# The order of a state-space mixer's block: weighted values and the next x's transposes behind the gate, the store behind the convolution

## The chip, the cores and the metric

The kernel runs on one core of a Trainium2 chip. The metric is the device time of one execution in microseconds, taken as the median of several runs. Five engines work side by side: TensorE (PE in the profile, with its weight loads as PEld), VectorE (DVE), ScalarE (ACT), GpSimd (POOL) and SyncE (SP). Each engine takes its instructions in the order in which they stand in its queue, and waits on semaphores for what other engines and DMA transfers produce. In this kernel SyncE issues nearly all transfers, and ScalarE's queue issues one kind, the store of a block's result.

## The reference

The network is one layer of four parts: causal attention with 32 heads and an adapter, a gated linear layer ("ffn"), a state-space mixer, and the ffn again, each behind a layer norm and added to x. The input is (4, 256, 512) in float32. The change lies in the mixer, which is cut here to what matters:

```python
proj = input_states @ in_proj_w.T             # gate 8192, x 8192, B 1024, C 1024, dt 128
xBC = silu(causal_conv4(xBC) + conv_b)        # four taps per channel
dt = softplus(dt + dt_bias); cum = cumsum(dt * A)
# 128 heads of 64; B and C are shared by the 16 heads of a group (8 groups)
y = (C B^T, causal, times exp(cum_i - cum_j)) @ (dt * x) + D * x
g = y * silu(gate)
g = g * rsqrt(mean over the group's 1024 channels of g*g + eps) * norm_w
out = g @ out_w.T
```

## The kernel before

Channels are taken 128 at a time: a block is two heads, 64 blocks in all (`NB`), eight to each of eight groups (`GB`, `G`). In block i, g is its group and gi its place in the group. All 1024 tokens (four sequences of 256) lie along the free axis, so a block's arrays are 128x1024.

A large product is done as three products of split operands (`mm3`, lines 115 to 117: upper by upper, upper by lower, lower by upper). An upper part is a cast on ScalarE, a lower part a subtraction on VectorE; both are named "lowering" and "copy" below.

The function `block(i)` (line 1513) issues the work of one block. Nothing is planned by costs: the instructions stand on each engine in the order in which the code calls them. The steps, with the names of the profile:

- x projection: 24 matmuls into `pp`, in two halves of 12 (`projected("x", i)`).
- `decays(i - 1)`: on ScalarE the exponentials of the decays of the block before, in `em` (lines 1205 to 1213), after which the next rows of cumulated sums are fetched (`rows`, L1178).
- `turn(i - 1)`: eight transposes of the former block's x on TensorE into two PSUM banks (`trx`, L1225), multiplied by dt on VectorE into `xd` (L1228). It stands between the two halves of the x projection.
- `weigh(i - 1)`: VectorE multiplies `em` by the scores `gm` (L1218).
- `conv` and `taps`: ScalarE's first tap (L962), then three on VectorE (L972).
- `squared(i - 2)`: the square of an older result on ScalarE (L1274, L1276), added up on GpSimd (L1277).
- `outer`: 24 matmuls of the output product of the group before, for one tile of tokens (`pog`), in blocks that have one; VectorE adds the result to x (`scaled`, L1373).
- `side_by_side`: the SiLU of the convolution (L1144), which makes the block's x; it needs a table load on ScalarE first.
- `inner_products(i - 1)`: `product`, 32 pairs of small matmuls into `pyy` (L1244), and `finish`, which is `gated` on VectorE (L1256, L1259): the block's result `gb`.
- gate projection: 24 matmuls, then `gate(i)` on ScalarE (L1435).
- `differences(i)` on VectorE (L1193, L1194): the exponents for the next block's `decays`.

In blocks with an output product ahead of the gate, `inner_products(i - 1)` stands between that product and the gate projection; in others (group 0, the first block of group 1, and each second block, gi = 1) it stands behind the gate projection.

The result `gb` is stored in DRAM (`spilled(i - 2)`, L1265) by ScalarE's queue at the head of block i, and read back (`fetch_half`, `gr`, L1341, on SyncE's queue) once a group is whole. In the second block of a group the last block of the former group is stored; the read-back of its half waits for that store. In the same block that half is cast (`upper_half`, L1351), four blocks of output weights are copied (`upper_out`, L1298, from `wor`, L1291), and behind the block the sums of squares (`pqs`, L1314), the first output product and a small transpose (`trq`, L1326) follow on TensorE. In ScalarE's queue the cast and the copies stand ahead of the block's `side_by_side`:

```python
if g and gi >= 1:
    ss = {1: (1,), 2: (4, 5)}.get(gi, (2 * gi, 2 * gi + 1))
    lower.extend(upper_half(g - 1, s) for s in ss)
if g and gi == 1:
    lower.extend(upper_out((g - 1) * GB + k) for k in range(4, 8))
g_steps = projected("g", i)
xs2[i] = side_by_side(acc)
```

In the fourth and fifth blocks (gi = 3, 4) the B and C projections of the next group follow the gate (24 matmuls each); in the seventh (gi = 6) the next group's scores are made (`scores`, `pg`, L1162).

PSUM has eight banks: four for two `pp`, two for `pyy`, and two shared by `trx`, `pog`, `pg`, `pqs` and `trq` (tag "m"). There is one `xd`, so a block's xd can be written only when the former product has read it.

Of the kernel before, what the change touches and what calls it, by code (L numbers as in the profile page):

```python
# [79 lines left out]
def hybrid_kernel(  # L80
# [788 lines left out]
    def mixer(feed, ps, mnorm, later):  # L869
        with ExitStack() as es, ExitStack() as inner:  # L870
# [391 lines left out]
            def spilled(n, gb):  # L1262

                if n < NB - 1:
                    nc.scalar.dma_start(spill[(n // GB) % 2][n % GB], gb)  # L1265
                else:
                    last.append(gb)

            def squared(n, x2, gb):

                g = n // GB
                if g not in sqs:
                    sqs[g] = p2.tile([P, NT], F32, name="sq", tag="sq", bufs=1)
                    nc.scalar.activation(sqs[g], gb, AF.Square)  # L1274
                else:
                    nc.scalar.activation(x2, gb, AF.Square)  # L1276
                    (nc.gpsimd if n < NB - 2 else nc.vector).tensor_tensor(sqs[g], sqs[g], x2, ALU.add)  # L1277
# [130 lines left out]
            def fetch_half(q, s):  # L1408
                halves[q, s] = recall(q, s // 2, s % 2)
# [20 lines left out]
            xs2, gts, ems, xds, gbs = {}, {}, {}, {}, {}  # L1430
# [10 lines left out]
            def turn(i):  # L1441
                xds[i] = turned(i, xs2[i])
# [5 lines left out]
            def inner_products(i):  # L1448
                finish(i, product(xds.pop(i), ems.pop(i)))

            def finish(i, py):
                gbs[i] = gated(i, xs2[i], gts.pop(i), py)
# [60 lines left out]
            def block(i):  # L1513

                g, gi = divmod(i, GB)
                n = at["x", i]
                lower = []  # L1520

                def lowered():
                    for f in lower:
                        f()
                    lower.clear()

                out = (g - 1, gi - 1) if gi else (g - 2, TT - 1)
                if out[0] < 0:  # L1530
                    out = None
                first_out = gi == 1

                if i >= 2:
                    spilled(i - 2, gbs[i - 2])
                if g and gi == 1:
                    fetch_half(g - 1, 1)
                    fetch_half(g - 1, 2)
                if late_:
                    nc.vector.reciprocal(rgs[g - 1], rgs[g - 1])  # L1540
                    scaled(*late_.pop())
                if g and gi == 2:
                    upper_half(g - 1, 3)()
                x_steps = projected("x", i)
                next(x_steps)
                pp = next(x_steps)
                waiting = [k for k in "bc" if k + "pp" in group]

                def begun_next(k):
                    group[k] = conv(group[k + "pp"], (NB if k == "b" else NB + G) + g + 1, False)  # L1550

                def ended_next(k):
                    taps(group[k], group.pop(k + "pp"), (NB if k == "b" else NB + G) + g + 1)


                for k in waiting if g == 0 else ():
                    begun_next(k)
                    ended_next(k)


                between = out is None
                decays(i - 1, (0,) if between else (0, 1))
                for k in waiting if g else ():
                    begun_next(k)
                turn(i - 1)
                if between:
                    weighted(ems[i - 1][0], gms[(i - 1) // GB])
                else:
                    weigh(i - 1)
                for k in waiting if g else ():  # L1570
                    ended_next(k)
                next(x_steps)
                acc = conv(pp, i, True)
                if between:
                    decays(i - 1, (1,))
                    taps(acc, pp, i, which=(0, 1))
                    weighted(ems[i - 1][1], gms[(i - 1) // GB])
                    taps(acc, pp, i, which=(2,))
                else:
                    taps(acc, pp, i)  # L1580
                if i >= 2:
                    squared(i - 2, xs2.pop(i - 2), gbs.pop(i - 2))
                done = outer(*out) if out and not first_out else None
                lower.append(upper_piece(n + 2))
# [7 lines that stand above are left out]
                for k in waiting:  # L1592
                    silu(group[k])
                if done:
                    scaled(*done)
                lowered()

                both = i == NB - 1
                scoring = None

                def scored():
                    nonlocal scoring
                    if gi == 6 and g + 1 < G:
                        scoring = scores(group.pop("b"), group.pop("c"))
                        gms[g + 1] = next(scoring)
                        next(scoring)
                        next(scoring)

                next(g_steps)
                for _ in pending:  # L1610
                    for _ in pending.pop():
                        pass
                if done and not both:
                    inner_products(i - 1)
                    pp = next(g_steps)
                    scored()
                    next(g_steps)
                else:
                    pp = next(g_steps)
                    next(g_steps)  # L1620
                    scored()
                    if both:
                        return last_block(i, pp)
                    inner_products(i - 1)
                lower.append(upper_piece(n + 3))
                if g and gi == 0:
                    lower.append(upper_half(g - 1, 0))
                    lower.extend(upper_out((g - 1) * GB + k) for k in range(4))
                if g and gi == 1:
                    lower.append(upper_half(g - 1, 2))  # L1630
                ems[i] = [differences(h) for h in (2 * i, 2 * i + 1)]
                lowered()
                if scoring and g:
                    for _ in scoring:
                        pass
                elif scoring:
                    pending.append(scoring)
                if gi == 6:
                    for k in range(4):
                        fetch_out(g * GB + k)  # L1640
                if g == 0 and gi == 7:
                    fetch_half(0, 0)
                gate(i, pp)
                if g and first_out:
                    r = sums(g - 1)
                    late_.append(outer(*out))
                    rgs[g - 1] = root(sums_turned(r))
                if gi in NEXT and g + 1 < G:
                    group[NEXT[gi] + "pp"] = whole(projected(NEXT[gi], g + 1))
                    upper_piece(n + 4)()  # L1650
# [13 lines left out]
            def last_block(i, pp):  # L1664

                g = i // GB
                py = product(xds.pop(i - 1), ems.pop(i - 1))
                done = outer(G - 2, TT - 1)
                for k in range(3):
                    fetch_out(NB - 3 + k)  # L1670
                ems[i] = [differences(h) for h in (2 * i, 2 * i + 1)]
                made(0, 0)()
                gate(i, pp)
                decays(i, (0,))
                lower = [upper_out(g * GB + k) for k in range(4)]
                lower.append(made(1, 0))
                for f in lower[:2]:
                    f()
                scaled(*done)
                for f in lower[2:]:  # L1680
                    f()
                weighted(ems[i][0], gms[g])
                finish(i - 1, py)
                decays(i, (1,))
                made(2, 0)()
                turn(i)
                weighted(ems[i][1], gms[g])
                spilled(i - 1, gbs[i - 1])
# [6 lines left out]
            i = NB - 1  # L1695
# [208 lines left out]
```

## Time and profile before

| what | value |
|---|---|
| median of 3 runs | 1811.24 us (1810.67 to 1813.12) |
| profiled execution, its own time | 1812.82 us |
| its span, first to last instruction | 1811.0 us |
| mean granted TensorE clock | 0.994 |
| PE busy | 1754.1 us, 97% of the span |
| DVE busy | 1439.5 us, 79% |
| ACT busy | 1268.4 us, 70% |
| POOL busy | 250.9 us, 14% |
| moved by DMA | 169.51 MB, mean 94 GB/s |

The table comes from the page of the profile. Busy time of an engine is the time in which it has an instruction in hand; matmuls overlap, so 97% says that there is always one in flight. A timeline row gives the start, the duration, the engine, the source line, the operation, the tiles (out<-in), the shape, how many instructions are merged, and in brackets the idle time before it and what ended that. The letter q behind an engine's name marks its queue, which issues transfers.

### The profile page before, as it was taken

How to read it: one execution, taken by the hardware profiler on the slowest of the kernel's cores; microseconds unless marked ns; L12 is line 12 of the kernel's file. 1: busy time of each engine (PE TensorE's matmuls, PEld its weight loads, DVE VectorE, ACT ScalarE, POOL GpSimd, SP SyncE). 2: the span in 40 equal slices, each digit the busy share in tenths (PEclk: the TensorE clock that was granted, in tenths of full speed). 3: DMA queues.
4: the chain of work that ended last, by engine and by line, in shares of the span. 5: the costliest groups of instructions: out<-in, count | busy, mean ns of one | idle time of the engine just before them, and what ended most of it. 6: DMA issues, size and time to landing. Idle time of an engine off the chain costs nothing.

```text
span 1811.0 us, 32937 instructions
## 1 busy us (share of the span) xinstructions
PE 1754.1 (97%) x12734; PEld 1425.0 (79%) x12734; DVE 1439.5 (79%) x2547; ACT 1268.4 (70%) x2289; POOL 250.9 (14%) x253
## 2 busy tenths in 40 slices
PE   8999988899999999999999999999999999999998
PEld 6777767778877888888888888888888888888877
DVE  6676677888998788878878797878787878887777
ACT  6666675487888667766866686768667866777754
POOL 6332230110110011011101111110111001101100
PEclk9999999999999999999999999999999999999999
DMA  4000000113243334423432343335323433343231
GB/s 151 1 1 1 23 15 26 43 59 106 94 134 125 105 94 135 134 76 103 162 109 93 94 146 99 100 94 170 99 93 104 154 105 94 111 140 112 85 98 57
DMA packets 134381, 169.51 MB, mean 94 GB/s; under 512 B 12240, under 2 KB 77520, under 8 KB 134224
## 3 DMA queue, kind: packets, MB, share of 16 engines
q1 hardware_dynamic: 125152, 134.37, 24.3%
q10 hardware_dynamic: 9072, 33.03, 4.8%
q8 instruction: 100, 1.64, 0.4%
q14 instruction: 57, 0.47, 0.1%
HBM read 131.71 MB, written 35.65 MB: 92 GB/s over the span
## 4 chain that ended last, share of the span: by engine, by line
PE 79%; DVE 10%; ACT 7%; issue 2%; POOL 1%; DMA 1%; SPq 0%; ACTq 0%; DVEq 0%; POOLq 0%
PE pp L115 14%; PE pp L117 13%; PE pp L116 13%; PE pyy L1244 8%; PE pog L115 6%; PE pog L116 6%; PE pog L117 6%; PE trx L1225 3%; PE ptr L521 1%; ACT e L505 1%; DVE acc L972 1%; PE pq L115 1%; PE pg L1162 1%; PE pq L116 1%; DVE eT L522 1%
## 5 line engine op out<-in xcount | busy, mean ns | idle before, releaser
L115 PE MATMUL pp<-mx,w 128*128 128x512 f32 x1144 | 459.3, 401 | 0.0
L117 PE MATMUL pp<-mx,w 128*128 128x512 f32 x1144 | 446.7, 391 | 0.0
L116 PE MATMUL pp<-mx,w 128*128 128x512 f32 x1144 | 446.1, 390 | 0.0
L1277 POOL TENSOR_TENSOR sq<-sq,x 128x1024 f32<-128x1024 f32 x54 | 132.1, 2446 | 1177.8 <-ACT x L1276 1177.8
L117 PEld LDWEIGHTS pp<-mx,w 128*128 128x128 f32 x1144 | 214.8, 188 | 46.2
L115 PEld LDWEIGHTS pp<-mx,w 128*128 128x128 f32 x1144 | 214.8, 188 | 44.6
L972 DVE SCALAR_TENSOR_TENSOR acc<-pp,cw_s,acc 128x1012 f32<-128x1012 f32 (+2 forms) x192 | 244.6, 1274 | 4.3
L116 PEld LDWEIGHTS pp<-mx,w 128*128 128x128 f32 x1144 | 215.2, 188 | 40.4
L1218 DVE TENSOR_TENSOR em<-em,gm 128x1280 f32<-128x1280 f32 x128 | 189.5, 1489 | 72.1 <-ACT em L1213 72.1
L115 PE MATMUL pog<-wo,gh 128*128 128x512 f32 x512 | 200.7, 392 | 1.9 <-DVE x L1373 1.9
L117 PE MATMUL pog<-wo,gh 128*128 128x512 f32 x512 | 199.7, 390 | 0.9 <-DVE gh L1356 0.9
L116 PE MATMUL pog<-wo,gh 128*128 128x512 f32 x512 | 199.4, 389 | 0.0
L1228 DVE TENSOR_TENSOR xd<-trx,dt_t 128x512 f32<-128x512 f32 x128 | 82.4, 686 | 141.4 <-PE trx L1225 141.4
L1144 ACT ACT_TABLE_LOAD x63 | 80.8, 1283 | 138.8 <-DVE acc L972 138.7
L1435 ACT ACTIVATE gt<-pp 128x1024 f32<-128x1024 f32 x64 | 65.6, 1025 | 145.2 <-PE pp L117 145.2
L1244 PEld LDWEIGHTS pyy<-em,xd 64*64 64x64 f32 x4096 | 130.2, 133 | 44.2 <-issue 17.3
L1205 ACT ACTIVATE em<-r,end_t 128x128 f32<-128x128 f32 x512 | 163.0, 389 | 0.8
L1244 PE MATMUL pyy<-em,xd 64*64 64x256 f32 (+3 forms) x4096 | 157.8, 300 | 3.1 <-DVE em L1218 2.9
L115 PEld LDWEIGHTS pog<-wo,gh 128*128 128x128 f32 x512 | 96.1, 188 | 24.7 <-issue 2.7
L117 PEld LDWEIGHTS pog<-wo,gh 128*128 128x128 f32 x512 | 96.1, 188 | 22.2 <-DVE gh L1356 2.1
L116 PEld LDWEIGHTS pog<-wo,gh 128*128 128x128 f32 x512 | 96.1, 188 | 19.4
L505 ACT ACTIVATE e<-e,nmx 128x256 f32<-128x256 f32 (+1 forms) x256 | 96.6, 450 | 19.9 <-DVE nmx L496 19.3
(323 smaller groups left out, 3131.8 us busy)
## 6 DMA issues: line engine op xcount, KB each, us to landing
wr<-in_win_dram SPq DMA_DIRECT2D x144, 256.0 KB, 2.8
r<-cumd SPq DMA_DIRECT2D x256, 128.0 KB, 2.9
spill<-gb ACTq DMA_DIRECT2D x63, 512.0 KB, 2.8
gr<-spill SPq DMA_DIRECT2D x120, 256.0 KB, 3.5
wor<-in_wout_dram SPq DMA_DIRECT2D x64, 256.0 KB, 4.5
out_dram<-x SPq DMA_DIRECT2D x7, 256.0 KB, 2.6
x<-in_x_dram SPq DMA_DIRECT2D x1, 1536.0 KB, 8.8
gr<-spill SPq DMA_DIRECT2D x8, 192.0 KB, 2.5
```

The costliest lines, as they stand in the source:

```text
L115: nc.tensor.matmul(o, lh, rh, start=(first and k == 0), stop=False)
L116: nc.tensor.matmul(o, lh, rl, start=False, stop=False)
L117: nc.tensor.matmul(o, ll, rh, start=False, stop=(last and k == n - 1))
L505: nc.scalar.activation(es_[c][:, 2 * j + pr, :], es_[c][:, 2 * j + pr, :], AF.Exp, scale=-1.0, bias=nm[:, j : j + 1],)
L972: nc.vector.scalar_tensor_tensor(av[:, :, d:], pv[:, :, : L - d], cw_s[:, ch, tap : tap + 1], av[:, :, d:], ALU.mult, ALU.add,)
L1144: nc.scalar.activation(pair(x2).rearrange("p k u i -> p u k i"), acc.rearrange("p (u k i) -> p u k i", u=2, i=Q), AF.Silu,)
L1205: nc.scalar.activation(piece(e, j, c, 2 - c, 2), rv[:, j, 2:, :], AF.Exp, bias=end_t[:, 2 * j + c, h : h + 1],)
L1218: nc.vector.tensor_tensor(e, e, gm, ALU.mult)
L1228: nc.vector.tensor_tensor(xd[:, hs, :].rearrange("p c (h d) -> p c h d", h=2), tr.rearrange("p c (h d) -> p c h d", h=2), dt_t[:, hs, 2 * ...
L1244: nc.tensor.matmul(py[d, u, j * L + c * Q : (j + 1) * L].rearrange("p (k i) -> p k i", i=Q), xd[us, 4 * j + c, d], piece(es2[hh], j, c)[us ...
L1277: (nc.gpsimd if n < NB - 2 else nc.vector).tensor_tensor(sqs[g], sqs[g], x2, ALU.add)
L1435: nc.scalar.activation(gts[i], pp, AF.Silu)
```

## The change

Three things change in `block`. First, `turn` is called for the block's own x at the end of the block, directly behind `product(i - 1)`, rather than for the former block's x between the halves of the x projection. Second, `product(i - 1)` stands behind the whole gate projection in every block, and `finish` behind `turn`; on VectorE the order at the end of a block is now `differences`, the xd products, the gating. Third, the store of block i - 2, and in each second block the two read-backs behind it, are called behind the taps; on ScalarE's queue the store then stands directly behind the convolution, ahead of the square.

```diff
-                if i >= 2:
-                    spilled(i - 2, gbs[i - 2])
-                if g and gi == 1:
-                    fetch_half(g - 1, 1)
-                    fetch_half(g - 1, 2)
                 if late_:
...
-                turn(i - 1)
+                if i == 2:
+                    turn(i - 1)
                 if between:
...
                     taps(acc, pp, i)
                 if i >= 2:
+                    spilled(i - 2, gbs[i - 2])
+                    if g and gi == 1:
+                        fetch_half(g - 1, 1)
+                        fetch_half(g - 1, 2)
                     squared(i - 2, xs2.pop(i - 2), gbs.pop(i - 2))
...
-                if done and not both:
-                    inner_products(i - 1)
-                    pp = next(g_steps)
-                    scored()
-                    next(g_steps)
-                else:
-                    pp = next(g_steps)
-                    next(g_steps)
-                    scored()
-                    if both:
-                        return last_block(i, pp)
-                    inner_products(i - 1)
+                pp = next(g_steps)
+                next(g_steps)
+                scored()
+                if both:
+                    return last_block(i, pp)
+                py = product(xds.pop(i - 1), ems.pop(i - 1))
...
                 ems[i] = [differences(h) for h in (2 * i, 2 * i + 1)]
+                turn(i)
+                finish(i - 1, py)
                 lowered()
```

## The prediction

> **What bounds the kernel now.** I read the page first, then the timeline of TensorE in a plain block of the mixer, then ScalarE, SyncE and TensorE in the block where a group's sums fall due.
>
> ```profile
> PE 1754.1 (97%) x12734; PEld 1425.0 (79%) x12734; DVE 1439.5 (79%) x2547; ACT 1268.4 (70%) x2289; POOL 250.9 (14%) x253
> PE 79%; DVE 10%; ACT 7%; issue 2%; POOL 1%; DMA 1%; SPq 0%; ACTq 0%; DVEq 0%; POOLq 0%
> ```
>
> TensorE (PE) is busy for 97% of the span and carries 79% of the chain that ended last. There is little idle time to win back: the question is whether the new order opens holes in it.
>
> ```profile
> 910.76 0.39 PE L117 MATMUL pog<-wo,gh 128*128 128x512 f32 x1
> 911.08 2.41 PE L1244 MATMUL pyy<-em,xd 64*64 64x256 f32 x64
> 913.42 0.50 PE L115 MATMUL pp<-mx,w 128*128 128x512 f32 x1
> 913.75 0.39 PE L116 MATMUL pp<-mx,w 128*128 128x512 f32 x1
> ...
> 921.49 0.40 PE L117 MATMUL pp<-mx,w 128*128 128x512 f32 x1
> 921.72 1.04 PE L1225 MATMUL trx<-con,x 128*128 128x128 f32 x8
> 922.51 0.48 PE L115 MATMUL pp<-mx,w 128*128 128x512 f32 x1
> 922.83 0.40 PE L116 MATMUL pp<-mx,w 128*128 128x512 f32 x1
> ```
>
> Large matmuls start every 0.227 us without a break. The weighted values (L1244) and the transposes (L1225) are two inserts between them.
>
> The third reading is the second block of group 3 (i=25). Its x projection starts at 878.48 on TensorE. Call that s.
>
> ```profile
> 878.74 0.33 ACTq L1265 DMA_DIRECT2D spill<-gb  x1
> 886.36 1.19 ACT L962 ACTIVATE acc<-pp,cb_s,cw_s 128x1024 f32<-128x1024 f32 x1
> 889.29 0.62 ACT L1351 CAST gh<-gr 128x512 fp32r<-128x512 f32 x1 [0.28 <-DMA gr<-spill]
> 889.82 2.56 ACT L1298 ACTIVATE wo<-wor,nw_s 128x512 fp32r<-128x512 f32 x4
> 892.39 1.28 ACT L1144 ACT_TABLE_LOAD   x1
> 893.68 1.06 ACT L1144 ACTIVATE x<-acc 128x1024 f32<-128x1024 f32 x1
> ```
>
> ```profile
> 879.59 2.31 SPq L1291 DMA_DIRECT2D wor<-in_wout_dram  x4
> 882.73 0.93 SPq L1341 DMA_DIRECT2D gr<-spill  x2
> ```
>
> ```profile
> 890.35 2.41 PE L1244 MATMUL pyy<-em,xd 64*64 64x256 f32 x64
> 892.69 0.64 PE L1314 MATMUL pqs<-sq,ones 128*32 128x256 f32 x8
> 898.98 0.47 PE L115 MATMUL pp<-mx,w 128*128 128x512 f32 x1
> ```
>
> The last block of the former group is stored (spill), read back (gr), and cast (L1351); only behind that cast and four copies of output weights does ScalarE compute the SiLU that makes x, ending at 894.74, s+16.26. The read-back ended ScalarE's wait already: it has no slack here. TensorE has, because it transposes this x only in the next block, at 901.82.
>
> **The change, part by part.**
>
> *The two inserts made neighbours.* Now: pog to pyy 0.32, pyy to pp 2.34, first pp 0.33; pp to trx 0.23, trx to pp 0.79, first pp 0.32: 4.33 over six steps. Together: 0.32 + 2.34 + 0.79 + 0.32 = 3.77 over four, and two ordinary steps of 0.227: 4.22. That is 0.106 us saved in each of the 47 blocks that have an output product ahead of the gate: -5.0. No row shows pyy directly before trx; the bounds are 0 and that saving. [...]
>
> *Waits that vanish.* The view of L1225's waits has "DVE x L1373: 4.3, 4": transposes that found no free PSUM bank behind the late output product. They now run before that product: -4.3 (0 to -4.3).
>
> *Plain blocks (those 47).* x(i) is now transposed at the end of block i, after 72 large matmuls (16.34) and pyy (0.09 + 2.34): s+18.8, where s is always the block's first x matmul. Before, SiLU ended at s+15.9 (914.83 against 898.98). It comes earlier now: the gate no longer waits for pyy, so it starts some 3 us before s, and gate, table load and exponentials (0.93, 1.29, 5.33) end by s+4.5. What moves on VectorE: the two xd products (done at s+1.55) and the gating (2.6) stand ahead of one lowering (0.6), weighing (2.8) and taps (3.75, begun at 908.50): taps end at s+11.3, and SiLU, 1.29 and 1.06 later, at s+13.7. No wait, with 5 us of cover; without the cover each 1 us would cost 47.
>
> *Second blocks (gi=1), groups 2 to 7: the cost.* There is no output product ahead of the gate, so TensorE wants x after 48 matmuls (10.90), 0.09 and 2.34: s+13.33. SiLU is nowhere near. The store now stands behind the convolution on ScalarE's queue. x's last matmul is readable 0.42 after its issue, as the gate shows (918.77 to 919.19): 23 x 0.227 + 0.42 = s+5.64; the store follows by 0.06: s+5.70. Store to read-back issue takes 878.74 to 882.73 = 3.99: s+9.69. Behind the read-back on SyncE's queue stand later weight loads, which have time. Read-back to cast took 6.56 here; the page's median for gr is 3.5. The four loads of 256 KB that stood ahead of it still do, so I take 5.3: s+15.0. Cast to SiLU's end is 889.29 to 894.74 = 5.45: s+20.45. The transposes wait 7.1 (with 3.5 and 6.56: 5.3 and 8.4), and all behind them on TensorE: the sums, the output product, the next block. Then pqs (L1314) needs a PSUM bank that both transposes hold until xd is written; xd's first half starts 0.64 behind the transposes (921.72 to 922.36) and takes 0.64, against 0.79 of transposes: +0.6. Six blocks x 7.7 = +46.2 (35 to 54).
>
> [...]
>
> *Second block of group 1.* Block 8 has no output product, so ScalarE is behind when block 9 starts: SiLU's end s-1.0, two copies 1.0, four weight copies 2.56, gate 0.93, table load 1.29, exponentials 5.33: convolution at s+10.1. Then 0.06 + 3.99 + 5.3 + 5.45: s+24.9. The rest of the block (0.79, 0.6, 0.57 for pqs, 5.45, 0.3) ends at s+32.6; before it took 23.29 (527.83 to 551.12): +9.3 (5 to 12).
>
> *Group 0.* Blocks there have no output product (48 matmuls, 10.90, and 3.4 for the inserts), so x decides: x projection 5.64, convolution to SiLU's end 432.17 to 441.31 = 9.14, 0.1, transposes 0.79: 15.67 a block. Seven with two extra projections of 5.45 make 120.6 against 118.03 (421.83 to 539.86): +2.6 (-2 to +6).
>
> *Seventh blocks.* The second half of the scores needs the banks that the transposes hold: +0.6 in groups 1 to 6: +3.6 (0 to 5).
>
> *TensorE's clock.*
>
> ```profile
> 247.00:249.00 2.00, 0.04 (x1) 0.00 (x0) 0.00 (x0) 2.00 (x7) 0.00 (x0) 1.00 0.00 0
> 249.30:252.60 3.30, 3.30 (x18) 2.86 (x18) 2.47 (x7) 0.85 (x2) 0.00 (x0) 0.50 0.00 0
> ```
>
> These stretches (columns: PE busy first, granted clock third from the end) are of the attention: 2.19 us without a matmul, then the granted clock is 0.50, and back at 1.00 by 252.8. At half clock 3.4 us lose 1.7. Seven waits of 7 us or more ought to bring this: +11.9 (0, or 24 if the stretch is twice as long). [...]
>
> Sum: -5.0 - 4.3 + 46.2 + 9.3 + 2.6 + 3.6 + 11.9 = +64.3. The profiled execution took 1812.82 (span 1811.0, 1.8 around it), so 1877.1; it stood 1.58 over the median of 1811.24, so 1875.5 against the median. I say 1875.
>
> **The rivals.** *The store is not what ends last.* If the read-back lands early, VectorE still sets SiLU: from s, xd to 1.55, gating to 4.15, three lowerings (0.6, 0.6, 2.65) to 8.0, weighing to 10.8, taps to 14.5, table and SiLU to 16.9. The wait is 3.5, so six blocks at 4.1 and group 1 at 5 make 29.6; with -9.3, +2.6, +3.6 it is +26.5: 1838, or 1850 with the clock's 11.9. For it: by the page store and read-back land in 2.8 and 3.5 at the median. Against: the cast already waited for the read-back.
>
> *Faster.* TensorE wants x in a second block at s+13.33; if SiLU ends by then, nothing waits, and the saved seams and bank waits remain: -9.3, 1802. It decides at the cast: it must start by s+7.9, and the store leaves ScalarE at s+5.70 at the earliest. For it only the earlier gate; against it the 3.99 of the store alone.
>
> *x late in every block.* VectorE is 79% busy; if xd and the gating ahead of the weighing pushed taps out by over 5 us, every plain block would wait, at 1 us each 47 more: about 1922. Against: the steps that VectorE has in such a block add up to some 15.5 us of the 19.8 between its last output matmuls (910.76 to 930.55).
>
> **How the numbers follow.** Forecast 0.72, store not last 0.13, x late everywhere 0.07, faster 0.05, cancelling to nothing 0.03. With every term at its lower or upper bound at once the forecast would be 1840 or 1912; the range 1838 to 1900 takes in the first rival and most of the forecast's, and leaves out some 0.2. About 0.2% (3.6 us) is what this measurement can tell from no change: faster 0.05, same 0.03, slower 0.92.
>
> **What would show it.** Right: in the second block of each group TensorE's largest wait, by transposes (L1225) for x (ACT L1144), about 7 us; casts (L1351) waiting for gr; a granted clock below 1 there; plain blocks still without holes, some 0.1 us shorter. Wrong: transposes that start at s+13.4 in second blocks, or waits of them in plain blocks, or a second-block wait of 3.5 with no wait for gr.

## The result, and the profile after

The changed kernel takes 1870.65 us at the median (1865.88 to 1872.15), the kernel before 1811.47 in the same series (four runs, three of them those of the table above): a ratio of 1.0316 (95% interval 1.0301 to 1.033). The change costs 59 us; 64 were predicted. The profiled execution took 1869.54, with a span of 1867.8 and a mean granted clock of 0.981 (0.994 before).

The page first: the busy line and the chain of the changed kernel.

```profile
PE 1760.0 (94%) x12734; PEld 1431.6 (77%) x12734; DVE 1438.7 (77%) x2547; ACT 1273.3 (68%) x2289; POOL 265.7 (14%) x253
PE 71%; DVE 11%; ACT 10%; DMA 4%; issue 3%; POOL 1%; SPq 0%; ACTq 0%; DVEq 0%; POOLq 0%
```

TensorE has the same number of instructions and nearly the same busy time (1754.1 before), spread over a longer span. Of the chain it has lost 8 of 79 points, to ScalarE (7 to 10), DMA (1 to 4), VectorE and issue: TensorE now stands still while others finish. The view of waits of the changed kernel (total us, times, longest) says for what:

```profile
PE trx L1225 <- ACT x L1144: 50.2, 11, 9.0
ACT gh L1351 <- DMA gr<-spill: 43.0, 9, 5.8
```

Before, the view had no line like the first, and the second had 4.3 us. The block to read is again the second block of group 3; its x projection starts at s = 896.68. ScalarE, SyncE and TensorE in the timeline of the changed kernel:

```profile
902.46 1.21 ACT L962 ACTIVATE acc<-pp,cb_s,cw_s 128x1024 f32<-128x1024 f32 x1 [0.65 <-PE pp L117]
902.52 0.33 ACTq L1265 DMA_DIRECT2D spill<-gb  x1
...
910.56 0.62 ACT L1351 CAST gh<-gr 128x512 fp32r<-128x512 f32 x1 [5.43 <-DMA gr<-spill]
911.09 2.56 ACT L1298 ACTIVATE wo<-wor,nw_s 128x512 fp32r<-128x512 f32 x4
913.66 1.28 ACT L1144 ACT_TABLE_LOAD   x1
914.95 1.06 ACT L1144 ACTIVATE x<-acc 128x1024 f32<-128x1024 f32 x1
```

```profile
906.65 0.93 SPq L1341 DMA_DIRECT2D gr<-spill  x2
```

```profile
907.79 2.41 PE L1244 MATMUL pyy<-em,xd 64*64 64x256 f32 x64
916.06 1.97 PE L1225 MATMUL trx<-con,x 128*128 128x128 f32 x8 [5.86 <-ACT x L1144]
918.05 1.08 PE L1314 MATMUL pqs<-sq,ones 128*32 128x256 f32 x8
```

This is the predicted sequence: store behind the convolution, read-back 4.13 us later, cast 3.91 after that with ScalarE idle for 5.43, four copies, table load, SiLU, and only then the transposes; TensorE has waited 5.86 for them. The next block starts at s+28.57, against s+20.50 before. The clock follows in the windows view (length, then busy time of PE, PEld, DVE, ACT and POOL, granted clock, DMA share, GB/s):

```profile
910.20:916.00 5.80, 0.00 (x1) 0.00 (x0) 5.80 (x10) 5.41 (x8) 0.00 (x0) 0.77 0.56 159
916.10:921.00 4.90, 4.88 (x22) 3.37 (x23) 4.43 (x7) 3.51 (x5) 0.00 (x0) 0.59 0.39 138
```

VectorE is busy through the whole wait (5.80 of 5.80). What it does there turns out to matter as much as the read-back.

### The profile page after: what moved, and what is told of

Same layout as the page of the kernel before. It is cut to its first block, busy times and chain, and to the rows that moved or that the text cites. A ratio compares the mean times of both kernels' runs of the same rounds, so it can differ in the third digit from the quotient of the medians.

```text
span 1867.8 us, 32972 instructions
## 1 busy us (share of the span) xinstructions
PE 1760.0 (94%) x12734; PEld 1431.6 (77%) x12734; DVE 1438.7 (77%) x2547; ACT 1273.3 (68%) x2289; POOL 265.7 (14%) x253
## 4 chain that ended last, share of the span: by engine, by line
PE 71%; DVE 11%; ACT 10%; DMA 4%; issue 3%; POOL 1%; SPq 0%; ACTq 0%; DVEq 0%; POOLq 0%
PE pp L115 12%; PE pp L116 11%; PE pp L117 11%; PE pyy L1244 6%; PE pog L115 5%; PE pog L116 5%; PE pog L117 5%; PE trx L1225 3%; DMA spill<-gb 2%; DMA gr<-spill 1%; ACT e L505 1%; ACT wo L1298 1%; DVE acc L972 1%; PE ptr L521 1%; ACT L1144 1%
## 5 line engine op out<-in xcount | busy, mean ns | idle before, releaser
L1277 POOL TENSOR_TENSOR sq<-sq,x 128x1024 f32<-128x1024 f32 x54 | 146.4, 2712 | 1219.4 <-ACT x L1276 1219.4
L117 PEld LDWEIGHTS pp<-mx,w 128*128 128x128 f32 x1144 | 215.0, 188 | 46.2
L1193 DVE TENSOR_TENSOR em<-r,col_t 128x512 f32<-128x512 f32 x128 | 88.0, 687 | 180.4 <-PE pyy L1244 179.8
L962 ACT ACTIVATE acc<-pp,cb_s,cw_s 128x1024 f32<-128x1024 f32 x64 | 77.2, 1207 | 114.2 <-PE pp L117 114.0
L1225 PE MATMUL trx<-con,x 128*128 128x128 f32 x512 | 76.2, 296 | 51.7 <-ACT x L1144 50.2
L115 PEld LDWEIGHTS pog<-wo,gh 128*128 128x128 f32 x512 | 97.3, 190 | 27.6 <-DVE xd L1228 5.7
L117 PEld LDWEIGHTS pog<-wo,gh 128*128 128x128 f32 x512 | 96.7, 189 | 22.3 <-DVE gh L1356 2.1
```

Source lines behind the costliest of these rows:

```text
L115: nc.tensor.matmul(o, lh, rh, start=(first and k == 0), stop=False)
L117: nc.tensor.matmul(o, ll, rh, start=False, stop=(last and k == n - 1))
L962: nc.scalar.activation(acc[:, cs], pp[:, cs], AF.Identity, bias=cb_s[:, ch : ch + 1], scale=cw_s[:, ch, 3:4])
L1193: nc.vector.tensor_tensor(own, rv, cv.to_broadcast([P, 2, 4, Q]), ALU.subtract)
L1225: nc.tensor.transpose(trs[c // 4][:, c % 4, :], x2[:, c * P : (c + 1) * P], ident)
```

## The experiments

Theory A is the prediction's: the read-back holds the cast on ScalarE, the cast holds SiLU, and TensorE waits for x. Its rivals are told in the expectations; the one that mattered, theory C, came out of the first runs: VectorE's queue is as late as ScalarE's. Unless a diff says otherwise it is against the changed kernel. The experiments ran in four series, each with the kernel before beside it (medians 1812.0, 1813.06, 1812.18 and 1813.69); the ratios are against these, and medians of different series are comparable to some 2 us. "Second block" without more is that of group 3; sums are over the seven second blocks (146.3 us before, 205.0 changed).

**1. The transposes of second blocks as late as before.** Only these blocks' own x is transposed in the following block.

```diff
-                if i == 2:
+                if i == 2 or (g and gi == 2):
                     turn(i - 1)
...
-                turn(i)
+                if not (g and gi == 1):
+                    turn(i)
```

> The changed kernel, but in each second block (gi = 1, groups 1 to 7) the block's own x is transposed in the next block, between the halves of the x projection, as before. Store, products and all other blocks stay as changed. Theory A (the loss is the wait of those seven transpositions, and nothing else): the sums and the output product run at once behind the weighted values; their casts and weight copies (911.09 to 914.98 in the changed kernel) are just in time for the product's second half, so a second block takes about 20 us instead of 28.3 to 33.3, the whole gain comes back less some bank waits: 1812 (1808 to 1820), with the clock never at half in the mixer. Theory B (the late store itself is the loss, wherever x is transposed): the output product waits for the read-back instead, 3 us or more a block: 1835 or more.

Measured: 1833.73, ratio 1.0122 (1.0099 to 1.0145). 37 of the 59 us come back, not all. The cast still waits 5.44 for gr, but no longer in front of TensorE's next work. What is late next stands in TensorE's timeline of this kernel:

```profile
907.45 0.53 PE L1326 MATMUL trq<-con,rows__10170 128*128 128x128 f32 x2 [1.85 <-ACT rows__10170 L1319]
```

ScalarE copies the group's sums (L1319) behind SiLU and the gate, so the late read-back still delays the small transpose at the end of the block. With 21.80 the second block stays 1.3 over before, and the third, which now holds two transposes, is longer too (22.22 against 20.02). In groups 1, 3 and 6 part of that is the clock, which fell to half there for 3.41 us against the expectation (the mean granted clock is 0.991 against 0.994 before, some 11 us more at half; in group 3 the large matmuls from 908.21 to 910.34 start every 0.43 us in place of 0.227); in the other four the third blocks take 20.9 to 21.3. Moving the transposes into that block is the larger half of the loss; the late cast costs something in the old order also.

**2. SiLU ahead of the cast and the copies, in second blocks.**

```diff
                 lower.append(upper_piece(n + 2))
+                if g and gi == 1:
+                    xs2[i] = side_by_side(acc)
                 if g and gi >= 1:
...
-                xs2[i] = side_by_side(acc)
+                if i not in xs2:
+                    xs2[i] = side_by_side(acc)
```

> The changed kernel, but in second blocks ScalarE computes the SiLU that makes x ahead of the cast of the read-back and of the four weight copies. Theory A: x then ends at the taps' end plus table load and SiLU, 911.17 + 1.29 + 1.06 = 913.5 in the profile's group 3, where it was 916.0; the transposes wait 3.4 us instead of 5.9, the output product finds its weights lowered in time, and the seven blocks give 2.5 each, perhaps 1 more by a shorter stretch at half clock: 1853 (1845 to 1858). Theory B (the store is the whole loss): with no wait for the read-back ahead of x, all comes back: 1815.

Measured: 1888.43, ratio 1.0418 (1.0395 to 1.0441): 18 us slower than the changed kernel where a gain was expected. TensorE, then VectorE, of this kernel:

```profile
915.85 1.37 PE L1225 MATMUL trx<-con,x 128*128 128x128 f32 x8 [3.49 <-ACT x L1144]
922.32 1.08 PE L1314 MATMUL pqs<-sq,ones 128*32 128x256 f32 x8 [5.11 <-DVE xd L1228]
```

```profile
916.34 0.69 DVE L1356 TENSOR_TENSOR gh<-gr,gh 128x512 fp32r<-128x512 f32 x1 [2.37 <-ACT gh L1351]
916.96 2.74 DVE L1301 SCALAR_TENSOR_TENSOR wo<-wor,nw_s,wo 128x512 fp32r<-128x512 f32 x4
...
921.49 1.28 DVE L1228 TENSOR_TENSOR xd<-trx,dt_t 128x512 f32<-128x512 f32 x2
```

The transposes do start earlier (wait 3.49). But xd, which frees the PSUM banks for the statistics (pqs), stands on VectorE behind the lowerings of the very cast and copies that were put off, and behind the differences. Each us of earlier transposes was handed on to the next wait, with more: the statistics start 2.1 later than in the changed kernel and the block is 3.2 longer. The rest is probably the clock: the mean granted clock of the profiled execution is 0.974, 0.981 in the changed kernel, which makes some 98 us at half clock in all against 71, and from 923.93 to 924.78 large matmuls of this block start 0.42 to 0.43 us apart in place of 0.227. The wait for xd is theory C.

**3. The new order with the store at the head of the block, and 4. the old order with the store behind the taps.** Experiment 3 takes the third part of the change back, experiment 4 is that part alone, in the kernel before.

```diff
+                if i >= 2:
+                    spilled(i - 2, gbs[i - 2])
+                if g and gi == 1:
+                    fetch_half(g - 1, 1)
+                    fetch_half(g - 1, 2)
                 if late_:
...
                 if i >= 2:
-                    spilled(i - 2, gbs[i - 2])
-                    if g and gi == 1:
-                        fetch_half(g - 1, 1)
-                        fetch_half(g - 1, 2)
                     squared(i - 2, xs2.pop(i - 2), gbs.pop(i - 2))
```

> The changed order of products and transposes, but the store and the two read-backs stay at the head of the block as before. Theory A (the order brings the loss; the store was moved because the gating now ends 4 us into the next block): the store at the head of ScalarE's queue waits for the gating at s+4.0 and holds the exponentials behind it. Second blocks: read-back issued at s+8.2 but the convolution only at s+12, so x ends at about s+19, as late as now. Group 0: convolution 2.6 later in each of seven blocks, +18. In all 1887 (1875 to 1900), slower than the changed kernel. Theory B (the late store is the loss): about 1838 or less.

> The kernel before, with only the store and the read-backs moved behind the convolution. Theory A: x is transposed one block later here, at s+23.3, and ends at about s+21.4 even with the read-back late (cast about 5 us later); the output product's second half waits some 0.5 us for its weights and the next block's exponentials start some 3 us later, about 1 us a second block: 1818 (1812 to 1826). Theory B (the late store is the loss): +50 or more, 1860.

Measured: the order alone 1920.64, ratio 1.0602 (1.0577 to 1.0627); the store alone 1820.42, 1.0046 (1.0033 to 1.006). So +108.6 for the order, +8.4 for the store, and +59 for both: the parts do not add. In the old order the later store costs a little, as expected: second blocks take 157.6 us, third blocks and group 0 give some back. In the new order the later store saves 50. ScalarE of the order alone, same block, s = 915.59:

```profile
919.52 0.33 ACTq L1265 DMA_DIRECT2D spill<-gb  x1
926.58 1.19 ACT L962 ACTIVATE acc<-pp,cb_s,cw_s 128x1024 f32<-128x1024 f32 x1
929.12 0.61 ACT L1351 CAST gh<-gr 128x512 fp32r<-128x512 f32 x1
```

The gating now stands behind the differences and xd on VectorE, so a store at the head of ScalarE's queue waits for it until s+3.9, and the exponentials and the convolution (s+11.0 in place of s+5.8) wait behind the store. The cast here waits for no read-back (no bracket), and yet TensorE waits 3.97 for x and 1.89 for xd: the block is longer (31.75) than in the changed kernel (28.57). The store in itself is not what makes the new order slow.

**5. The read-back off the path.** Half 1 of the group's result is replaced by a weight tile, which is there early; so this kernel leaves that half of the result out of the output product.

```diff
             def fetch_half(q, s):
-                halves[q, s] = recall(q, s // 2, s % 2)
+                if s == 1:
+                    halves[q, s] = po_.tile([P, 4, P], F32, name="gr", tag="gr", bufs=2)
+                    load(halves[q, s], win[0])
+                else:
+                    halves[q, s] = recall(q, s // 2, s % 2)
```

> The changed kernel, but the half that waits for the last store is not read back in second blocks: a weight tile of the same 256 KB, which nothing writes, is loaded in its place, so the values are not the reference's. Theory A (the read-back behind the late store sets the second block): ScalarE's cast waits no more, SiLU ends with the taps at s+16.8 instead of s+19.3, and seven blocks give 2.5 each: 1853. Theory C (after silu_first: VectorE's queue is as late by itself, since three lowerings of 3.9 and the differences of 2.05 stand between the taps at s+14.5 and the xd products, which free the PSUM bank that the sums wait for): the transposes start 2.5 earlier, but the sums wait for xd as long as before, and nothing is gained beyond 0.5 a block: 1868 (1862 to 1871).

Measured: 1872.32, ratio 1.0329 (1.0312 to 1.0346): no gain at all. TensorE of this kernel, s = 891.70:

```profile
908.72 1.97 PE L1225 MATMUL trx<-con,x 128*128 128x128 f32 x8 [3.49 <-ACT x L1144]
912.71 1.08 PE L1314 MATMUL pqs<-sq,ones 128*32 128x256 f32 x8 [2.02 <-DVE xd L1228]
```

The transposes start at s+17.0 rather than s+19.4, the statistics at s+21.0 rather than s+21.4. VectorE, busy without a gap, has the lowerings (3.85 us) and the differences (1.88) between the taps and xd:

```profile
906.15 0.68 DVE L912 TENSOR_TENSOR w<-wr,w 128x512 fp32r<-128x512 f32 x1
906.75 0.69 DVE L1356 TENSOR_TENSOR gh<-gr,gh 128x512 fp32r<-128x512 f32 x1
907.36 2.73 DVE L1301 SCALAR_TENSOR_TENSOR wo<-wor,nw_s,wo 128x512 fp32r<-128x512 f32 x4
910.00 0.69 DVE L1193 TENSOR_TENSOR em<-r,col_t 128x512 f32<-128x512 f32 x1
...
911.88 1.28 DVE L1228 TENSOR_TENSOR xd<-trx,dt_t 128x512 f32<-128x512 f32 x2
```

The read-back, which ended the longest wait, was one of two chains of nearly the same length. In the changed kernel VectorE comes out just ahead of it, since xd waits there for the transposes:

```profile
917.22 0.69 DVE L1228 TENSOR_TENSOR xd<-trx,dt_t 128x512 f32<-128x512 f32 x1 [0.28 <-PE trx L1225]
```

So VectorE's queue alone holds nothing back there either; no run cleared it alone. The total lies just above what theory C allowed (1871).

**6. SiLU early and the lowerings behind xd.** Experiment 2, and in second blocks VectorE's lowerings behind `turn`.

```diff
-                lowered()
+                if not (g and gi == 1):
+                    lowered()
...
                 turn(i)
+                if g and gi == 1:
+                    lowered()
                 finish(i - 1, py)
```

> silu_first, and in second blocks also the lowerings of the cast and the weights on VectorE behind the xd products. Theory C (both queues, each by itself, hold the second block): SiLU at s+16.9, xd 1 us behind, sums and output product at s+18.2, their second half finds its weights in time: the block takes 24.5 instead of 28.6, seven give 4 to 4.5 each: 1840 (1832 to 1850). Theory D (something else, as the number of waits or DMA traffic, holds it): above 1865.

Measured: 1852.62, ratio 1.0217 (1.0201 to 1.0234), against 1888.43 with SiLU alone. One call on VectorE moved is worth 36 us. TensorE and VectorE, s = 891.97:

```profile
908.99 1.97 PE L1225 MATMUL trx<-con,x 128*128 128x128 f32 x8 [3.49 <-ACT x L1144]
910.98 1.08 PE L1314 MATMUL pqs<-sq,ones 128*32 128x256 f32 x8
910.14 0.69 DVE L1228 TENSOR_TENSOR xd<-trx,dt_t 128x512 f32<-128x512 f32 x1 [1.76 <-PE trx L1225]
```

The statistics start without a wait at s+19.0, and VectorE now waits for the transposes. The total is 3 us above the expected range; the rest of the wait, 3.49, is still enough to halve the clock (0.51 granted from 910 to 915).

**7. The wait filled.** 20 multiplications of ones by ones in front of each second block's transposes, into the bank that they then overwrite, so that TensorE does not fall idle.

```diff
                 trs = [ps.tile([P, 4, P], F32, name="trx", tag="m") for _ in range(2)]
+                if n > GB and n % GB == 1:
+                    for _ in range(20):
+                        nc.tensor.matmul(trs[0][:, 0, :], ones, ones, start=True, stop=True)
```

> The changed kernel, with 20 small matmuls of ones by ones in each second block, on TensorE between the weighted values and the transposes, into the bank that the transposes then overwrite: TensorE is at work for some 4 us of its 6 us wait, which itself stays. Theory A (the granted clock of 0.50 behind the wait costs 1.7 to 2 a block): the clock stays at 1.00 and seven blocks give 2 each: 1858 (1853 to 1864). Theory B (the half clock costs nothing, since other engines set those stretches): 1870 or more.

Measured: 1865.08, ratio 1.0287 (1.027 to 1.0303): 5.6 us less than the changed kernel (7.2 with each against the kernel before of its series, 6.0 in the second blocks), where some 12 were expected. The mean granted clock is 0.990 (0.981 changed), some 37 us at half in all (71). The clock stayed whole in groups 2 and 4 to 7, whose second blocks take 27.3 to 27.4 (28.3 to 29.2 changed), and still fell in groups 1 and 3 (33.4 and 28.86). So half the clock costs 1.0 to 1.9 us a block here, 1.3 on the mean of the five groups.

**8 and 9. The fillings again, with 13 multiplications, where one queue or both are cleared.** Number 8 is experiment 5 with the filling, number 9 experiment 6 with it.

> A weight tile is read in place of half of the read-back, so the values differ from the reference's; 13 multiplications of ones by ones keep TensorE at work while the transposes wait. Theory C (VectorE's queue, with xd behind the lowerings and the differences, is as late as the read-back): the statistics start 21.0 us into the second block, as in the kernel that only fills the wait, the block takes 27.3 us and the total is about 1865 us (1861 to 1868). Theory A (the read-back alone sets the length, and without it the gain was lost only to half the clock): the second block takes 24.9 us and the total is about 1848 us.

> SiLU ahead of the cast and the copies, the lowerings behind xd, and 13 multiplications of ones by ones in the wait that is left. Theory C (two queues and the clock, no more): the transposes start about 17.0 us into the second block, the statistics at 18.3 us, the block takes about 25.0 us and the total is about 1849 us (1843 to 1852). If the clock is not what the version without the filling lost, the total stays at 1852 us or above.

Measured: number 8 takes 1871.37, ratio 1.032 (1.0304 to 1.0335). TensorE, s = 895.37:

```profile
912.39 1.09 PE L1228 MATMUL trx<-con,x 128*128 128x128 f32 x8 [0.40 <-ACT x L1144]
916.39 1.08 PE L1317 MATMUL pqs<-sq,ones 128*32 128x256 f32 x8 [2.90 <-DVE xd L1231]
```

The statistics start at s+21.02, as theory C said, and as in experiment 7, which has the read-back (21.01); transposes at full speed (1.09 us, against 1.97 at half clock in experiment 5) only lengthen the wait for xd, from 2.02 to 2.90. That second wait is not filled and the clock fell behind it (0.52 granted from 916.30 to 919.70), which fits a block of 28.76, where 27.3 was expected (in experiment 7 as short a fall made group 3's 28.86), and a total above the 1868 allowed.

Number 9 takes 1840.47, ratio 1.0146 (1.0129 to 1.0163), under the expected range. ScalarE and TensorE, s = 886.08:

```profile
900.69 1.28 ACT L1144 ACT_TABLE_LOAD   x1 [6.17 <-DVE acc L972]
```

```profile
903.10 1.09 PE L1228 MATMUL trx<-con,x 128*128 128x128 f32 x8 [0.40 <-ACT x L1144]
904.63 0.64 PE L1317 MATMUL pqs<-sq,ones 128*32 128x256 f32 x8 [0.44 <-DVE xd L1231]
```

The windows view has a granted clock of 1.00 from 897.00 to 910.90 in this block, which takes 24.86. Against experiment 6 the filling is worth 12.1 us, three times what the expectation gave it; second blocks account for 10.1 of it (175.0 against 185.1). What is left over before, 4.3 us a block in groups 2 to 7, is the change's own: SiLU waits for the taps, which VectorE does behind xd, gating and lowerings of the block before.

The kernels side by side, for the second block of group 3 (starts of transposes and statistics from s):

| kernel | transposes | statistics | block | seven blocks | median |
|---|---|---|---|---|---|
| before | in the next block | 14.2 | 20.50 | 146.3 | 1811.47 |
| changed | 19.4 | 21.4 | 28.57 | 205.0 | 1870.65 |
| changed, filled | 19.2 | 21.0 | 28.86 | 199.0 | 1865.08 |
| SiLU first | 17.0 | 23.5 | 31.81 | 223.8 | 1888.43 |
| no read-back | 17.0 | 21.0 | 30.14 | 205.9 | 1872.32 |
| no read-back, filled | 17.0 | 21.0 | 28.76 | 204.3 | 1871.37 |
| SiLU first, xd first | 17.0 | 19.0 | 27.08 | 185.1 | 1852.62 |
| the same, filled | 17.0 | 18.6 | 24.86 | 175.0 | 1840.47 |

**10 and 11. Is there something to keep?** In number 10, the kernel before, the store goes behind the taps in all blocks but the second ones. Number 11 adds the new order in five blocks of each group from the second on, where the changed kernel's transposes found x ready. The diffs are against the kernel before.

```diff
-                if i >= 2:
+                if i >= 2 and g and gi == 1:
                     spilled(i - 2, gbs[i - 2])
...
                 if i >= 2:
+                    if not (g and gi == 1):
+                        spilled(i - 2, gbs[i - 2])
```

```diff
+            def new(i):
+                return GB < i < NB - 1 and i % GB in (2, 3, 4, 5, 7)
...
-                turn(i - 1)
+                if not new(i - 1):
+                    turn(i - 1)
...
+                if new(i):
+                    pp = next(g_steps)
+                    next(g_steps)
+                    py = product(xds.pop(i - 1), ems.pop(i - 1))
...
+                if new(i):
+                    turn(i)
+                    finish(i - 1, py)
```

> The kernel before, with the store behind the convolution in all blocks but the second ones, where store and read-backs stay at the head. By store_only's blocks the later store shortened block 2 by 0.65, 3 by 0.67, 8 by 1.69 and 10 by 1.74, since at the head ScalarE's queue waited for the gating; and it cost 1 to 3 in second blocks alone, which is left out here: 1806.5 (1804 to 1810). If those blocks were shorter by chance: 1811.

> store_but_second, and the changed order of products and transposes in the blocks with gi 2, 3, 4, 5 and 7 of groups 1 to 7, where it made no waits. The seams saved 0.04 us a block in the changed kernel, 34 blocks: 1.4 below store_but_second, 1805; if the order's handing over between blocks costs more than that: 1806 to 1810.

Measured: 1810.71 against 1812.18, ratio 0.999 (0.9981 to 0.9999), and 1808.93, 0.998 (0.997 to 0.999). Both gain less than the 1806.5 and 1805 expected; number 11 lies in the range given for an order that costs something where old and new blocks meet. The later store helps in group 0 and at block 8 (blocks 2, 3 and 8 shorter by 0.66, 0.71 and 1.70). Of the new order in plain blocks next to nothing is left: in group 3 the third block is 0.74 longer, the eighth 0.72 longer, the seventh and the first of the next group 0.76 shorter each. That is mostly the transposes, which change sides where an old block meets a new one; it nearly cancels. Number 11 has the lowest median of this study, 0.2% under the kernel before; its 1.8 us on number 10 lie within the spread of their runs.

## Why the prediction was right, and where it was not

**Sign and place: right, and shown.** Second blocks carry nearly all of it. By the starts of the x projections, the changed kernel's terms against the predicted ones are:

| term | predicted | measured |
|---|---|---|
| second blocks, groups 2 to 7 | 46.2, and clock 10.2 | 48.7 with the clock |
| second block of group 1 | 9.3, and clock 1.7 | 10.0 with the clock |
| group 0 | 2.6 | 2.4 |
| seventh blocks | 3.6 | 3.5 |
| bank waits (measured: third blocks as a whole) | -4.3 | -3.8 |
| seams and the rest of the plain blocks | -5.0 | -2.3 |

The clock's 11.9 is split here by block. The sum comes to 64.3 against 58.5 for the measured rows, and 59.2 by the medians.

**The read-back was mis-sized.** From s the convolution came at 5.78 (5.64 predicted), the store at 5.84 (5.70), the read-back's issue at 9.97 (9.69). From there to the cast 5.3 was taken, between the 6.56 of one row and the page's median; it measured 3.91. The cast came at 13.88 in place of 15.0, and the wait was 5.86 in place of 7.1.

**The seam.** A plain block saved 0.04 in a group's first and fifth blocks, not 0.106; it lies between the two bounds given. Fourth blocks are 0.10 longer, sixth and eighth 0.2 shorter, which was not followed up. TensorE's timeline of the changed kernel, in the fourth block of the group:

```profile
961.23 0.39 PE L117 MATMUL pp<-mx,w 128*128 128x512 f32 x1
961.55 2.41 PE L1244 MATMUL pyy<-em,xd 64*64 64x256 f32 x64
963.89 1.09 PE L1225 MATMUL trx<-con,x 128*128 128x128 f32 x8
964.74 0.49 PE L115 MATMUL pp<-mx,w 128*128 128x512 f32 x1
```

0.32 and 2.34 were as predicted; from the first transpose to the next large matmul it was 0.85 here, not 0.79, which leaves some 0.04. x was ready, as forecast: no wait stands in these rows, and the rival of an x that is late in every block fell with them.

**The bank waits were read twice.** The 4.3 that the prediction took from its view counts matmuls and their weight loads, which wait side by side. TensorE's own waits for L1373 in the kernel before come to 1.9 in two places:

```profile
PE trx L1225 <- DVE x L1373: 1.9, 2, 1.5
```

The longer, 1.5, is in group 1's third block, and went; the shorter is in the last group and stayed. Group 1's third block is 1.95 shorter; the other six are 0.3 shorter each, for which this view has no wait. That the row comes to -3.8 is luck.

**The rival that the store is not what ends last** was priced at 1838 to 1850 and given 0.13. Its reading of SiLU was exact: without the read-back the wait is 3.49 (3.5 foreseen). Its price was wrong, because it stopped at SiLU. Experiments 5 and 8 show that the total does not move, since xd on VectorE holds the banks until the statistics start at s+21. Only with VectorE's queue cleared and the clock kept (number 9) does that price hold: 4.3 us a block in place of 4.1, and 1840.47. The prediction named ScalarE as the only holder and took the 0.6 between transposes and statistics as given; that VectorE would be almost as late was missed, and for the same reason the expectation of number 2 had the wrong sign. So the wait was read rightly, and its removal worth nothing: the forecast priced one of two chains whose statistics start at s+21.4 and s+21.0, and its total would have come out even with a read-back that lands at once. That much of the agreement is luck.

**The clock.** The drop was foreseen, in each group's second block. Its price of 1.7 was taken for 3.4 us of work at half speed, and measured 1.3 on the mean in experiment 7 and 1.4 (10.1 over seven blocks) between numbers 6 and 9. In the changed kernel the granted clock is at half for 6.83 us in each of groups 2 to 7; 2.76 of that in group 3 lie in the wait (913.30 to 916.06), where TensorE has nothing to do; the 24 that the prediction put on so long a stretch did not come.

**Misses of the experiments.** Besides number 2, number 1 shows that the transposes' place alone is not the whole loss, as I had expected. Number 3 was mis-sized (1887 expected): in the new order the store at the head delays the exponentials of every block in which ScalarE has no slack, so that group 0 and the fifth blocks (26.27 against 25.23) grow too. Numbers 5 to 10 lie up to 3.4 us outside the ranges given for them. That ScalarE's lack of slack is the reason in each of these blocks is argued from the one block shown.

## What to carry to other kernels

Before a consumer is moved up to its producer, follow every queue that the producer and the consumer's successor stand in: here the work that TensorE overtook was waiting on ScalarE behind a read-back and on VectorE behind lowerings. Clearing ScalarE's queue alone gained nothing (experiment 5) or lost 18 us (experiment 2), and clearing both gained 18. An order with special blocks (a group's end, a late output product) should be priced block kind by block kind, since 47 plain blocks at -0.04 weigh nothing against seven at +8. When a wait is removed and the time stays, look at the next wait of the same engine and at what its releaser did in between.

## What the runs showed of the hardware that was not expected

The half-clock stretches of the changed kernel in the mixer last 6.83 us (10.24 in group 1); in group 3 of experiments 5, 6, 7 and 8 the windows views give 10.3, 6.8, 3.4 and 3.4. All are close to multiples of 3.41; in the kernel before, the stretch of the attention that the prediction read lasts 3.41 (249.27 to 252.68). A wait of 3.49 us for x stands ahead of the fall in group 3 of experiments 5 and 6, whose mean granted clocks are 0.980 and 0.983. There the clock fell 3.4 and 2.5 us after TensorE's last work, and in the changed kernel 3.1; in the row that the prediction read, 2.19 us without a matmul stand ahead of a clock of 0.50.

Nor did the half clock cost the same everywhere. In group 3, experiment 5 with 10.3 us of it takes 1.38 more than experiment 8 with 3.4, and experiment 6 with 6.8 takes 2.22 more than experiment 9 with none. And in experiment 7 the clock falls in group 3 and not in group 4, with the same filling. The windows view has for each of the two a stretch of 3.41 us and the one that follows; TensorE is busy for 1.68 us of the first in group 3 and for 1.91 in group 4, and the granted clock of the second is 0.50 and 1.00:

```profile
912.48:915.89 3.41, 1.68 (x17) 1.22 (x18) 3.41 (x7) 3.27 (x5) 0.00 (x0) 1.00 0.93 279
915.89:919.30 3.41, 3.41 (x15) 2.20 (x8) 3.38 (x6) 1.66 (x2) 0.00 (x0) 0.50 0.15 57
1093.40:1096.81 3.41, 1.91 (x16) 1.48 (x14) 3.41 (x7) 3.40 (x5) 0.00 (x0) 1.00 0.99 302
1096.81:1100.22 3.41, 3.17 (x19) 2.34 (x20) 3.38 (x6) 2.04 (x3) 0.00 (x0) 1.00 0.21 79
```

Busy time goes by modelled ends of the matmuls. What decided between the two groups was not shown: no run moved a wait in time and left all else as it was.
